# Time and channel mix on one core: sums and statistics of gathered rows behind the widening on VectorE

## The chip, the cores and the metric

The kernel runs on one core of a Trainium2 chip. A core has five engines that work side by side, each through its own queue in order: TensorE (PE in the profile, with its weight loads as PEld), VectorE (DVE), ScalarE (ACT), GpSimd (POOL) and SyncE (SP, which here only issues DMAs). They wait for each other through semaphores. The metric is the device time of one execution in microseconds (us), lower is better. About 0.2% of it (4.6 us) is what a measurement of this kernel can tell from no change.

## The reference

Two transformer-like layers over `x` of 32 sequences x 256 tokens x 128 channels, all float32, with a layer norm after each of the four parts: relative attention, a mixture of 14 routed and 2 shared experts (top 2), the time and channel mix, and attention over the sequence axis with a second mixture of 8 experts. The change lies in the third part, which with the norms around it is:

```python
x  = _layernorm(x + moe0(x))              # moe0's two routed rows per token are gathered and summed here
xn = _ln(x, ln1_g, ln1_b); xp = shift(xn)
k, v, r = mix(xn, xp) @ Wk, ... @ Wv, sigmoid(... @ Wr)
wkv = scan over the tokens: a = ew*a + exp(k)*v;  b = ew*b + exp(k);  a / (b + 1e-8)
y  = x + (r * wkv) @ Wo
yn = _ln(y, ln2_g, ln2_b)
kk = square(relu((0.5*yn + 0.5*shift(yn)) @ Wfk))   # 128 -> 512 channels: the widening
x  = _layernorm(x + y + sigmoid(yn @ Wfr) * (kk @ Wfv))  # 512 -> 128: the narrowing
```

## The kernel before

The phases run one after the other: `rel_attention`, `load_weights`, `moe0`, `rwkv`, `seq_attention`, `moe1`. The change is in `rwkv` (time and channel mix, from about 1243 us to about 1590 us of the profiled execution). It works on 8 units of 4 sequences, which are 1024 tokens or 8 tiles of 128 tokens each (`UB`, `UT`). In the code unit `i` is `q`, the next one is `ahead`, the one after it `third`. The next phase attends over the sequence axis, so it needs every unit of this one.

The order of the work is written out by hand: under `tc.manual_schedule` for PE, Pool, DVE and Activation, each engine executes its instructions in the order in which the loop at the end of `rwkv` issues them. So a line of that loop is a place in four queues at once. One iteration issues, with the lines of the code:

- `keys(ahead)`, `normed(q)`, `weigh(ahead)`, `values(ahead)`: mixing matmuls (L1419, L1420), exponentials, and on VectorE two scans (L1434, L1447) and a reciprocal of 6.5 us (L1450).
- `late(2)`, `scaled(third)`, `receive(ahead)`, `second(q)`: norm of the second half, transposes (L253), and two adds `ys` on GpSimd (L1487), from which the widening reads.
- `enter(third)`, `join(ahead)` (two VectorE operations, L1459, L1460), `gated(q)` (matmuls `ps_rr`, L1497).
- `late(3)`, then `widen(q)`.
- `settle(units[i - 1])`, `leave(ahead)`, `late(2)`, `narrow(q)`.

What these steps are made of:

- `late(n)` takes n steps of `taken_in()`, which has 51 steps: 18 are taken before the loop, 7 in each iteration, and they run out with the `late(3)` of iteration 4. Step k issues two gathers on GpSimd for row tile k (indirect DMAs, L935; each takes a place on GpSimd of about 1.3 us), then sums on VectorE the two rows of tile k-3 into X (two scalar_tensor_tensor, L1381). The last three steps have no gathers. After the eighth tile of a unit come its statistics: eight pairs of bn_stats and bn_aggr on VectorE (L1334, L1335, here called bn), then `sd_c` and `r_c` on GpSimd (L1336, L1337). In iterations 2, 3 and 4 these statistics fall into `late(3)`: after its first, second and third step. In iterations 0 and 1 they fall into the first `late(2)`.
- `widen(q)` issues an add X+y of 128x1024 on GpSimd (L1504), then eight times a matmul of the widening (`ps_kk`, L1510), a relu on ScalarE (L1515) and a square. The squares of the even blocks are on ScalarE (L1519), the four of the odd blocks on VectorE (L1517).
- `settle` finishes norms: for the unit before (`x`) and for a unit whose statistics are new (`c`), four small VectorE operations each (L1343 to L1348), of which the first, `shift_c`, needs `r_c` of GpSimd; then eight activations each on ScalarE (L1354) and a power on GpSimd (L1349).
- `leave(ahead)` has 8 matmuls `ps_o` (L1468), the add y = X + ps_o on VectorE (L1472, two operations of 128x512), and statistics of y. `narrow(q)` has 32 matmuls `ps_f` (L1527). Both write into the same two PSUM buffers (pool `r_o`), so `ps_f` can't start before L1472 has read `ps_o`. Behind `ps_f` come the gate (L1532), X (L1533), the statistics of x, and the next iteration's first scan on VectorE.

SyncE issues no DMA in this loop.

Of the kernel before, what the change touches and what calls it, by code (L numbers as in the profile page):

```python
# [30 lines left out]
class Kernel:  # L31
# [1237 lines left out]
    def rwkv(self):  # L1269
        nc, tc = self.nc, self.tc  # L1270
        UB, UT = 4, 8
        with ExitStack() as ctx:
# [44 lines left out]
            for i in range(B // UB):  # L1317
                q = Unit()
# [73 lines left out]
            def late(n):  # L1392
                for _ in range(n):
                    next(steps, None)

            def settle(q=None):
                if q is not None:
                    s = slice(UT * q.i, UT * (q.i + 1))
                    finish("x", q.x, q.x, q.last, self.scale2[:, s])
                while norms:  # L1400
                    i, stats = norms.pop(0)
                    x, s = units[i].x, slice(UT * i, UT * (i + 1))
                    finish("c", x, x, stats, self.scale1[:, s])
                    ready.add(i)

            def scaled(q):
                assert q.i in ready
                q.h = two.tile([P, UT, D], F32, tag="ln1", name="ln_h1", bufs=1)
                for t in range(UT):
                    s0 = UT * q.i + t  # L1410
                    nc.scalar.mul(q.h[:, t, :], q.x[:, t, :], self.scale1[:, s0 : s0 + 1])

            def enter(q):
                q.xn = turned(q.i, "xn", q.h, c["ln1_g"], c["ln1_b"])
# [8 lines left out]
            def keys(q):  # L1423
                q.ek = two.tile([P, UB, N], F32, tag="ek", name="ek")
                for u in range(0, UB, 2):
                    ps = mixdot(q, "k", u)
                    nc.scalar.activation(q.ek[:, u : u + 2, 1:], ps[:, :, 1:], AF.Exp)
                    nc.scalar.activation(
                        q.ek[:, u : u + 2, 0:1], ps[:, :, 0:1], AF.Exp, bias=c["time_first"]
                    )  # L1430

            def weigh(q):
                sb = q.sb = two.tile([P, UB, N], F32, tag="sb", name="sb")
                nc.vector.tensor_tensor_scan(  # L1434
                    flat(sb), flat(ew), flat(q.ek), 0.0, ALU.mult, ALU.add
                )
                nc.vector.tensor_scalar(sb, sb, 1e-8, None, ALU.add)

            def values(q):
                ekv = two.tile([P, UB, N], F32, tag="ekv", name="ekv")  # L1440
                for u in range(0, UB, 2):
                    ps = mixdot(q, "v", u)
                    nc.vector.tensor_tensor(
                        ekv[:, u : u + 2, :], q.ek[:, u : u + 2, :], ps, ALU.mult
                    )
                q.sa = two.tile([P, UB, N], F32, tag="sa", name="sa")
                nc.vector.tensor_tensor_scan(  # L1447
                    flat(q.sa), flat(ew), flat(ekv), 0.0, ALU.mult, ALU.add
                )
                nc.vector.reciprocal(q.sb, q.sb)  # L1450

            def receive(q):
                q.rr = two.tile([P, UB, N], F32, tag="rr", name="rr")
                for u in range(0, UB, 2):
                    ps = mixdot(q, "r", u)
                    nc.scalar.activation(q.rr[:, u : u + 2, :], ps, AF.Tanh, scale=0.5)

            def join(q):
                nc.vector.scalar_tensor_tensor(q.sa, q.rr, 1.0, q.sa, ALU.add, ALU.mult)  # L1459
                nc.vector.tensor_tensor(q.sa, q.sa, q.sb, ALU.mult)  # L1460

            def leave(q):
                y = q.y = two.tile([P, UT, D], F32, tag="y", name="y")
                for t0 in range(0, UT, 4):
                    ps = ps_o.tile([P, 4, D], F32, tag="o", name="ps_o")
                    for t in range(4):
                        b, f = divmod(t0 + t, 2)
                        nc.tensor.matmul(  # L1468
                            ps[:, t, :], q.sa[:, b, P * f : P * (f + 1)], wo,
                            start=True, stop=True,  # L1470
                        )
                    nc.vector.tensor_tensor(  # L1472
                        y[:, t0 : t0 + 4], q.x[:, t0 : t0 + 4], ps, ALU.add
                    )
                mv, r, shift = q.stats = statistics("y", y)
                nc.gpsimd.tensor_tensor(shift, mv[:, :, 0], r, ALU.mult)
                nc.gpsimd.tensor_scalar(shift, shift, -1.0, None, ALU.mult)

            def normed(q):
                q.h2 = two.tile([P, UT, D], F32, tag="ln2", name="ln_h2", bufs=1)  # L1480
                apply(q.h2, q.y, q.stats)
# [9 lines left out]
            def gated(q):  # L1491
                q.gate = two.tile([P, UT, D], F32, tag="gate", name="gate")
                for t0 in range(0, UT, 4):
                    ps = ps_o.tile([P, 4, D], F32, tag="o", name="ps_rr")
                    for t in range(4):
                        b, f = divmod(t0 + t, 2)
                        nc.tensor.matmul(  # L1497
                            ps[:, t, :], q.yn[:, b, 1 + P * f : 1 + P * (f + 1)], m["Wfr"],
                            start=True, stop=True,
                        )  # L1500
                    nc.scalar.activation(q.gate[:, t0 : t0 + 4], ps, AF.Tanh, scale=0.5)

            def widen(q):
                nc.gpsimd.tensor_add(q.x, q.x, q.y)  # L1504
                q.kks = []
                for u in range(0, UB, 2):
                    kk = two.tile([P, 4, 512], F32, tag="kk", name="kk")
                    for k in range(4):
                        ps = ps_m.tile([P, 2, N], F32, tag="m", name="ps_kk")
                        nc.tensor.matmul(  # L1510
                            ps, wfk[:, P * k : P * (k + 1)], q.ys[:, u : u + 2, :],
                            start=True, stop=True,
                        )
                        ps = ps.rearrange("p b t -> p (b t)")
                        nc.scalar.activation(kk[:, k, :], ps, AF.Relu)  # L1515
                        if k % 2:
                            nc.vector.tensor_tensor(kk[:, k, :], kk[:, k, :], kk[:, k, :], ALU.mult)  # L1517
                        else:
                            nc.scalar.activation(kk[:, k, :], kk[:, k, :], AF.Square)  # L1519
                    q.kks.append(kk)  # L1520
# [16 lines left out]
            with tc.manual_schedule(engines={E.PE, E.Pool, E.DVE, E.Activation}):  # L1537
                late(11)
                scaled(units[0])
                enter(units[0])  # L1540
                keys(units[0])
                weigh(units[0])
                late(2)
                values(units[0])
                receive(units[0])
                scaled(units[1])
                enter(units[1])
                join(units[0])
                late(2)
                leave(units[0])  # L1550
                late(3)
                settle()
                for i, q in enumerate(units):
                    ahead = units[i + 1] if i + 1 < len(units) else None
                    third = units[i + 2] if i + 2 < len(units) else None
                    if ahead:
                        keys(ahead)
                    normed(q)
                    if ahead:
                        weigh(ahead)  # L1560
                        values(ahead)
                    late(2)
                    if third:
                        scaled(third)
                    if ahead:
                        receive(ahead)
                    second(q)
                    if third:
                        enter(third)
                    if ahead:  # L1570
                        join(ahead)
                    gated(q)
                    late(3)
                    widen(q)
                    settle(units[i - 1] if i > 0 else None)
                    if ahead:
                        leave(ahead)
                    late(2)
                    narrow(q)
                settle(units[-1])  # L1580
# [539 lines left out]
```

## Time and profile before

| | us |
|---|---|
| median of 3 runs | 2285.38 |
| lowest, highest run | 2281.87, 2285.68 |
| profiled execution, its time | 2282.96 |
| profiled execution, its span | 2281.3 |

| engine | busy us (share of the span) |
|---|---|
| PE | 1878.6 (82%) |
| DVE | 1303.4 (57%) |
| ACT | 1089.7 (48%) |
| POOL | 874.5 (38%) |

Busy time by iteration of the loop, from the windows view (each begins at a first scan of VectorE, to about a microsecond). Iterations 5 and later have no gathers, sums or such statistics left.

| iteration | us | PE | DVE | ACT | POOL | granted PE clock |
|---|---|---|---|---|---|---|
| 0 | 50 | 33.50 | 38.30 | 23.86 | 34.76 | 0.83 |
| 1 | 48 | 33.15 | 37.71 | 24.77 | 33.87 | 0.86 |
| 2 | 41 | 33.55 | 36.58 | 25.60 | 32.26 | 0.92 |
| 3 | 40 | 32.55 | 35.03 | 24.32 | 32.84 | 0.91 |
| 4 | 42 | 32.47 | 36.61 | 25.10 | 22.18 | 0.92 |
| 5 | 32 | 30.44 | 27.91 | 22.00 | 12.52 | 1.00 |

A line of the timeline reads: start in us from the span's start, duration in us, engine, line of the code, operation, what it writes and reads, shape, count; in brackets the idle time of the engine before it and what ended it. Instructions of one kind that follow each other are merged into one line. A line of the windows view has the stretch, its length, then for each engine the busy time and, in parentheses, the number of instructions, then the granted PE clock as a share of full speed, and DMA.

### The profile page before, as it was taken

Reading aid. Unit: us, or ns where it says so; the run is one execution under the profiler, and the core shown is the slowest. Engines: PE = TensorE matmul, PEld = TensorE weight load, DVE = VectorE, ACT = ScalarE, POOL = GpSimd, SP = SyncE. Lnnn points to the kernel's source line nnn. Section 1 sums busy time; section 2 is a strip of 40 time slices with the busy share of each in tenths; the row PEclk is TensorE's granted clock in tenths of the full one; section 3 lists DMA queues with packets and bytes.
Section 4 is the critical chain, followed back from the end, with each engine's and each line's share of the span. In section 5 each row is a group of like instructions: output and inputs, shape, how many; then the busy total and the mean of one; then the engine's idle time right before and its main releaser. Section 6 shows DMA issues by size and latency. Waiting matters only on the chain.

```text
span 2281.3 us, 57436 instructions
## 1 busy us (share of the span) xinstructions
PE 1878.6 (82%) x22616; PEld 1492.9 (65%) x22616; DVE 1303.4 (57%) x4578; ACT 1089.7 (48%) x2438; POOL 874.5 (38%) x1047
## 2 busy tenths in 40 slices
PE   3899999999887995897998578887677777499795
PEld 2788887887776874676987345555455534399663
DVE  2465666666755655522423878986576535444575
ACT  1566665565554552332376346655576322244231
POOL 4000011002135423485056667744301165453775
PEclk9899999999999996899998789999798766599898
DMA  5121233101111102112453000001000000155221
GB/s 169 23 70 24 57 106 106 49 13 48 42 42 31 30 21 58 55 45 67 133 139 106 23 23 21 21 1 38 1 3 21 20 36 35 47 162 160 77 60 58
DMA packets 190957, 127.93 MB, mean 56 GB/s; under 512 B 54114, under 2 KB 179043, under 8 KB 189155
## 3 DMA queue, kind: packets, MB, share of 16 engines
q1 hardware_dynamic: 175074, 93.79, 14.2%
q0 software_dynamic: 14336, 29.39, 4.1%
q8 instruction: 182, 2.98, 0.5%
q10 hardware_dynamic: 1280, 1.08, 0.2%
q14 instruction: 85, 0.69, 0.1%
HBM read 61.27 MB, written 62.91 MB: 54 GB/s over the span
## 4 chain that ended last, share of the span: by engine, by line
PE 24%; DVE 16%; POOL 13%; issue 9%; DMA 5%; ACT 4%; another core or an unknown queue 1%; SPq 0%; POOLq 0%; DVEq 0%; ACTq 0%
POOL rows L925 4%; PE ps_sh L1009 3%; PE ps_sy L1022 3%; DMA gy<-results,at 3%; PE ps_f L1527 3%; POOL gy L935 2%; PE ps_s L1712 2%; DMA y<-results,at 1%; DVE sb L1450 1%; PE ps_t L543 1%; POOL y L935 1%; POOL rstd L171 1%; POOL xs L1099 1%; ACT pbuf L532 1%; PE sc L503 1%
## 5 line engine op out<-in xcount | busy, mean ns | idle before, releaser
L503 PE MATMUL sc<-ke,qt 64*64 64x256 f32 (+15 forms) x8192 | 359.3, 315 | 32.1 <-DMA qt<-qd 18.2
L503 PEld LDWEIGHTS sc<-ke,qt 64*64 64x64 f32 x8192 | 330.0, 205 | 75.1 <-issue 50.6
L532 ACT ACTIVATE pbuf<-pbuf,nb 128x256 f32<-128x256 f32 (+15 forms) x1024 | 313.5, 395 | 132.0 <-DVE nb L528 132.0
L528 DVE CUSTOM_DVE_ANT_0 pbuf<-sc,mask 128x256 f32<-128x256 f32 (+15 forms) x1024 | 229.9, 295 | 68.9 <-PE sc L503 49.3
L543 PE MATMUL ps_t<-ident,pbuf 128*128 128x128 f32 x1560 | 201.1, 280 | 21.4 <-ACT pt L132 10.0
L132 ACT COPY pt<-ps_t 128x512 f32<-128x512 f32 x195 | 113.9, 586 | 195.6 <-PE ps_t L543 184.9
L543 PEld LDWEIGHTS ps_t<-ident,pbuf 128*128 128x128 f32 x1560 | 172.9, 143 | 40.7 <-ACT pt L132 12.2
L134 DVE COPY pt<-ps_t 128x512 f32<-128x512 f32 x195 | 134.5, 691 | 72.5 <-PE ps_t L543 67.3
L1009 PE MATMUL ps_sh<-sxt,w1t 128*128 128x128 f32 x1088 | 139.2, 282 | 23.8 <-DVE sxt L981 10.8
L590 POOL TENSOR_TENSOR X<-X,r_L_attn_bp 128x2048 f32<-128x2048 f32 x4 | 18.3, 4564 | 365.6 <-PE ps_x L400 365.6
L759 ACT ACTIVATE hid<-ps_h 128x512 f32<-128x512 f32 x128 | 76.0, 597 | 162.7 <-PE ps_h L755 146.7
L925 POOL DMA_INDIRECT rows<-xs,where x128 | 125.4, 979 | 72.3 <-issue 37.4
L1009 PEld LDWEIGHTS ps_sh<-sxt,w1t 128*128 128x128 f32 x1088 | 130.4, 196 | 28.4 <-DVE sxt L981 11.4
L1014 ACT ACTIVATE shid<-ps_sh 128x512 f32<-128x512 f32 x136 | 81.0, 597 | 126.8 <-PE ps_sh L1009 108.4
L935 POOL DMA_INDIRECT gy<-results,at x96 | 94.7, 986 | 48.4 <-DMA sx<-rows 20.7
L925 POOL DMA_INDIRECT rows<-X,at x96 | 94.5, 985 | 29.1 <-issue 15.1
L556 PE MATMUL av<-pt,v 128*32 128x256 f32 (+1 forms) x2048 | 97.8, 332 | 7.6 <-DVE pt L134 6.9
L935 POOL DMA_INDIRECT y<-results,at x64 | 63.7, 995 | 104.3 <-DMA results<-sy 85.7
L914 POOL COPY at<-where 128x1 int32<-128x1 int32 x256 | 51.7, 203 | 121.9 <-DVE where L899 54.2
L580 DVE RECIPROCAL rc<-ps_c 128x16 f32<-128x16 f32 x64 | 16.4, 257 | 131.4 <-PE ps_c L577 131.4
L528 DVE DVE_READ_ACCUMULATOR2_ANT nb<- 128x1 f32 x1024 | 85.1, 83 | 0.0
L1527 PE MATMUL ps_f<-wfv,kk 128*128 128x128 f32 x512 | 65.9, 295 | 22.9 <-DVE y L1472 22.9
(355 smaller groups left out, 3966.2 us busy)
## 6 DMA issues: line engine op xcount, KB each, us to landing
sx<-rows SPq DMA_DIRECT2D x68, 256.0 KB
results<-sy SPq DMA_DIRECT2D x68, 256.0 KB
rows<-zero SPq DMA_DIRECT2D x10, 1024.0 KB
qt<-qpd SPq DMA_DIRECT2D x512, 8.0 KB
qd<-st SPq DMA_DIRECT2D x4, 1024.0 KB
qpd<-sp SPq DMA_DIRECT2D x4, 1024.0 KB
qt<-qd SPq DMA_DIRECT2D x256, 16.0 KB
kd<-st SPq DMA_DIRECT2D x4, 1024.0 KB
```

What stands on the lines that cost most here:

```text
L132: self.nc.scalar.copy(out, in_)
L134: self.nc.vector.tensor_copy(out, in_)
L503: nc.tensor.matmul(s.bank[i][64 * f : 64 * f + 64, off : off + w], lhs, rhs, start=key not in s.seen, stop=(1 - rows, g, f) in s.seen, ski ...
L528: nc.vector.tensor_tensor_reduce(out=pr, in0=s.bank[i][:, off : off + w], in1=mask[:, N - w : N], scale=-QS, scalar=3e38, op0=ALU.add, op1 ...
L532: last = nc.scalar.activation(pr, pr, AF.Exp, bias=nb, scale=-1.0)
L543: nc.tensor.transpose(ps[:, k, :], s.prob[:, at : at + P], ident)
L556: nc.tensor.matmul(av[32 * bl : 32 * bl + 32, bh, P * f :], v[:, 2 * b + f, 9 * s.h : 9 * s.h + 32], ptv[:, 32 * f : (32 if f == 0 else 48 ...
L925: i = nc.gpsimd.indirect_dma_start(rows, bass.IndirectOffsetOnAxis(ap=at, axis=0), src[:, n, :], None)
L935: self.nc.gpsimd.indirect_dma_start(out, None, rows, bass.IndirectOffsetOnAxis(ap=where, axis=0))
L1009: nc.tensor.matmul(ps[:, t, c, :], w1[t2 + t][:, P * c : P * (c + 1)], xt[:, t2 + t, :], start=True, stop=True,)
L1014: nc.scalar.activation(h.rearrange("p (t c) n -> p t c n", t=2), ps, func)
L1527: nc.tensor.matmul(ps[:, t, :], kk[:, k, P * t : P * (t + 1)], wfv[:, k, :], start=(k == 0), stop=(k == 3),)
```

## The change

In the loop at the end of `rwkv`, `late(3)` changes its place with `widen(q)`:

```diff
                     gated(q)
+                    widen(q)
                     late(3)
-                    widen(q)
                     settle(units[i - 1] if i > 0 else None)
                     if ahead:
                         leave(ahead)
```

Nothing is added or removed. On VectorE the sums (and in iterations 2, 3 and 4 the statistics) now stand behind the four squares and directly in front of `settle`. On GpSimd the add X+y (L1504) now stands directly behind the two `ys` adds, in front of the six gathers and of `sd_c` and `r_c`. PE's and ScalarE's queues keep their order, since `late` issues nothing on them.

## The prediction

> **What bounds it now.** I read the shares of the page, then the chain of waits between 1243 and 1336 us, then the timeline of each engine for iterations 0 to 5. Over the whole kernel PE is busiest, but in this loop the chain of waits goes through VectorE and from there into the narrowing. The page's groups say what its matmuls wait for:
>
> ```profile
> L1527 PE MATMUL ps_f<-wfv,kk 128*128 128x128 f32 x512 | 65.9, 295 | 22.9 <-DVE y L1472 22.9
> ```
>
> All their idle time is ended by y (L1472) on VectorE. So what counts is when L1472 starts: each us by which it is later makes the iteration longer by one, because `ps_f`, gate, X, statistics and the next scan follow it in one row. There are two kinds of iteration. VectorE, GpSimd and ScalarE in iteration 0:
>
> ```profile
> 1312.18 0.69 DVE L1517 TENSOR_TENSOR kk<-kk 128x512 f32<-128x512 f32 x1 [2.96 <-ACT kk L1515]
> 1315.05 0.69 DVE L1517 TENSOR_TENSOR kk<-kk 128x512 f32<-128x512 f32 x1 [2.17 <-ACT kk L1515]
> 1317.05 3.06 DVE L1517 TENSOR_TENSOR kk<-kk 128x512 f32<-128x512 f32 x2 [1.31 <-ACT kk L1515]
> ...
> 1320.59 1.28 DVE L1472 TENSOR_TENSOR y<-X,ps_o 128x512 f32<-128x512 f32 x2
> ```
> ```profile
> 1316.57 2.39 POOL L1504 TENSOR_TENSOR X<-X,y 128x1024 f32<-128x1024 f32 x1
> ```
> ```profile
> 1318.16 0.58 ACT L1515 ACTIVATE kk<-ps_kk 128x512 f32<-128x512 f32 x1
> ```
>
> Here VectorE idles in front of the squares (2.96 + 2.17 + 1.31 us), waiting for relus: the sums in front of them cost nothing. The third square (3.06 for two, against 0.69 for one) is held up until the GpSimd add ends at 1318.96. Iteration 1 is alike (idle 4.35, 2.16, 1.30; two squares 3.08). Iteration 2, VectorE, ScalarE, PE:
>
> ```profile
> 1398.40 0.73 DVE L1381 SCALAR_TENSOR_TENSOR X<-y,gate,X 128x128 f32<-128x128 f32 x2
> ...
> 1402.23 1.36 DVE L1381 SCALAR_TENSOR_TENSOR X<-y,gate,X 128x128 f32<-128x128 f32 x4
> 1403.51 2.49 DVE L1517 TENSOR_TENSOR kk<-kk 128x512 f32<-128x512 f32 x4
> 1405.91 0.16 DVE L1343 SCALAR_TENSOR_TENSOR shift_x<-mv_x,r_x 128x8 f32<-128x8 f32 x1
> ...
> 1407.02 1.28 DVE L1472 TENSOR_TENSOR y<-X,ps_o 128x512 f32<-128x512 f32 x2
> ```
> ```profile
> 1401.44 0.58 ACT L1515 ACTIVATE kk<-ps_kk 128x512 f32<-128x512 f32 x1
> ```
> ```profile
> 1407.75 9.75 PE L1527 MATMUL ps_f<-wfv,kk 128*128 128x128 f32 x64 [4.88 <-DVE y L1472]
> ```
>
> VectorE is never idle from its first scan to y; the relus are done (1402.02) before the squares begin. Iterations 3 and 4 are alike.
>
> **The change, part by part.** Moved are, in iterations 0 to 4: six sums on VectorE (1.95 us, from six in iteration 4, 1479.43 to 1481.38); in 2 to 4 also eight bn pairs (3.18 us, 1399.05 to 1402.23) and `sd_c`, `r_c` on GpSimd; in 0 to 3 six gathers. Four squares take 2.40 us in a row.
>
> *Iterations 0 and 1.* With the add out of the way, the last square waits only for the last relu (1318.16 + 0.58 = 1318.74) and is done at 1319.4, against 1320.04: 0.65 us gained. Then the sums, 1.95, now lie between squares and y: **+1.3**. In iteration 1 the last relu ends at 1366.55, the squares at 1367.2 (1367.87 before): again **+1.3**.
>
> *The add on GpSimd* goes to right behind the `ys` adds. In iterations 0 and 1 that is at 1308.7 and 1356.6, where VectorE idles: free. In 2, 3 and 4 it is at 1394.9, 1435.3 and 1475.9, where VectorE begins four sums and the join, all with two SBUF inputs like the held-up square. In iteration 0 a sum that met the `ys` adds took 1.96 us in place of 0.35. I take it that one sum waits out the add: the join ends 2.25 us later. The lower bound is no delay, if the add slips in behind the join.
>
> *Iteration 2.* Join done at 1398.40 + 2.25 = 1400.65, squares to 1403.05 (the last relu, 1402.02, is in time), two sums 1403.7, bn 1406.85, four sums 1408.15, four operations of settle for x 1408.7. `shift_c` waits for `r_c`: from the end of bn to the end of `r_c` it was 2.24 us (1402.23 to 1404.47; 2.78 in iteration 4, where squares ran beside it), so 1409.1. That wait is new; the squares covered it. Behind it in VectorE's queue stand the rest of settle (0.55) and y: 1409.7 against 1407.02, **+2.7**. Without the add's delay squares wait for relus, and it is +2.3.
>
> *Iteration 3.* Statistics after the second step, so less stands between them and `shift_c`: join 1441.0, squares 1443.4, four sums 1444.7, bn 1447.9, `r_c` 1450.1, y 1450.7 against 1447.41: **+3.3** (+2.9 without the delay).
>
> *Iteration 4.* No gathers; statistics at the very end. Before, the add held up a small operation of settle (L1348, 2.28 us in place of 0.17); that goes, and the sums pay instead. Join 1481.7, squares 1484.1, sums 1486.0, bn 1489.2, `r_c` 1491.45, y 1492.05 against 1490.15: **+1.9** (+1.45).
>
> *The gathers* come one add (2.4 us) later, in iteration 2 the last four behind the late `r_c` (about 1409.3 to 1414.1, before 1404.7 to 1409.5). The first sum that reads these rows would be at about 1414.8; a row landed about 1.5 us behind its gather in iteration 0 (1305.34 to 1306.85), so they are there. On GpSimd behind them: `r_y` and `shift_y` by 1420.2, which ScalarE wants at about 1424.3; then four gathers to 1425.2, and the next `sd_x` is held up by the scan until 1427.0 anyway, as before. Were this cover (1.8 us) gone, `ys` and the widening would be late by as much. SyncE's queue has nothing here.
>
> *Sum of the order:* 1.3 + 1.3 + 2.7 + 3.3 + 1.9 = **+10.5 us** (9.25 if the add is not in the way).
>
> *PE's clock.* In iterations 0 and 1 `ps_f` ran at full clock (7.42 us) behind idle gaps of 1.72 and 2.29 us. These grow to 3.0 and 3.6. The windows view, in pairs of neighbouring stretches:
>
> ```profile
> 863.10:866.50 3.40, 0.48 (x16) 0.13 (x4) 1.30 (x14) 3.40 (x13) 0.00 (x0) 1.00 0.00 0
> 866.50:869.90 3.40, 3.22 (x15) 3.22 (x16) 1.24 (x3) 0.43 (x2) 0.00 (x0) 0.51 0.00 0
> 1149.90:1153.30 3.40, 1.51 (x13) 1.51 (x14) 0.00 (x0) 2.15 (x6) 1.95 (x2) 1.00 0.33 96
> 1153.30:1156.70 3.40, 3.40 (x18) 3.40 (x18) 1.19 (x4) 2.56 (x7) 2.32 (x4) 0.50 0.23 67
> ...
> 1368.30:1371.70 3.40, 2.00 (x18) 2.00 (x18) 3.16 (x15) 3.40 (x10) 3.12 (x2) 1.00 0.00 0
> 1371.70:1375.10 3.40, 3.40 (x33) 3.40 (x32) 3.19 (x14) 2.62 (x7) 1.66 (x3) 1.00 0.00 0
> ```
>
> A stretch with PE busy for 0.48 or 1.51 us is followed by half clock; one with 2.00 (the gap of iteration 1) is not. The Trainium skill, "TensorE: Matmul & The Clock Gate", section "What's actually happening", says that the clock halves after an idle window of about 3.4 us, with windows that run freely. By that rule a gap of 3.0 us never fills a window and one of 3.6 hardly ever: cost 0, sum 10.5. By the rows partly busy windows are enough: in this trace all nine gaps of 2.7 to 6 us that began at full clock were followed by half clock, and of seven of 1.9 to 2.1 us three were. I go by the rows: both `ps_f` fall. The price is between 1.7 (3.4 us at half rate) and 2.6 (`ps_f` took 9.17, 9.75 and 10.03 in iterations 4, 2, 3); I take 2.0 each, **+4.0**. The widening's matmuls in 2 to 4 start behind gaps of 2.04 to 2.07 us and kept full clock three times; the squares now follow the relus closely, so a fall costs 1.7 less a slack of 0.4 (last relu at 1402.0, its square due at 1402.45). With three of seven such gaps falling, one of these three is likeliest: **+1.3**, ends 0 and 3.9.
>
> **Total:** 10.5 + 4.0 + 1.3 = **+15.8**. On the profiled execution (span 2281.3 and 1.7 around it: 2282.96) that is 2298.8. This execution lies 2.4 below the median of 2285.38 and inside the runs' spread; on the spread's middle, 2284, it is **2300**.
>
> **The rivals.**
> - *The clock holds* (26%): the order costs 9.25 to 10.5 and no fall is added: 2294. For it: the page's rule. Against: the nine gaps.
> - *Only places change* (10%): in iterations 2 to 4 VectorE was full, and swapping what fills it moves y by nothing; iterations 0 and 1 remain, +2.6, 2287, no change that can be told. For it: no idle time there. Against: it needs `r_c` in time, and squares, sums, bn and settle give no cover of 2.24 us after bn.
> - *The sums leave the path* (4%): faster. If y is issued without the sums and statistics in front of it, L1472 stands right behind squares and settle: by the same times -0.65 twice, -2.8, -2.9 and -4.9, together -12, and three `ps_f` behind gaps of about 2 us keep full clock, -6.6: 2266 to 2272. It decides where VectorE takes y ahead of sums that were issued before it. Against: in every iteration its order is the written one, and y starts within 0.1 us of the operation written before it.
> - *GpSimd late too* (8%): widening falls to half clock in two or three iterations, or gathers push `ys` back: 2304 to 2310.
>
> The forecast, order and both falls, +12 to +19, has 52%. Slower are it, the first and the last rival: 86%; same 10%, faster 4%. The range 2289 to 2307 leaves out the second and third rival and the top of the last.
>
> **What would show it.** Squares behind the join with 2.4 us in a row in iterations 2 to 4, a first sum of over 2 us beside L1504, no square above 0.7 us; `shift_c` idle for 0.4, 1.0 and 1.7 us behind `r_c`; gaps before `ps_f` of about 3.0, 3.6, 7.6, 8.2, 8.9; `ps_f` above 9 us in iterations 0 and 1. The prediction is wrong if y starts no later behind the join than before, or if `ps_f` no longer waits for y.

## The result, and the profile after

The changed kernel takes 2295.37 us (median of 5 runs, 2290.15 to 2300.93), the kernel before 2285.38 (5 runs, 2280.10 to 2286.76). The ratio is 1.0054, with a 95% interval of 1.0037 to 1.0072: slower by about half a per cent. The profiled execution of the changed kernel took 2290.15 us, its span is 2287.6.

The narrowing's group on the profile page, after; its idle time in front was 22.9 us before:

```profile
L1527 PE MATMUL ps_f<-wfv,kk 128*128 128x128 f32 x512 | 66.7, 297 | 32.5 <-DVE y L1472 32.5
```

In front of the narrowing PE waits 9.6 us longer, and for nothing but y. The windows view of the changed kernel, one line for each of iterations 0 to 4, cut at the first scan (L1434) of each:

```profile
1280.40:1331.74 51.34, 34.61 (x147) 24.05 (x146) 35.28 (x84) 22.47 (x50) 33.55 (x29) 0.80 0.09 24
1331.74:1383.17 51.43, 35.31 (x153) 22.87 (x152) 35.69 (x90) 25.26 (x58) 34.19 (x27) 0.83 0.07 18
1383.17:1425.31 42.14, 31.97 (x153) 21.39 (x152) 38.05 (x90) 24.99 (x58) 31.19 (x26) 0.92 0.07 20
1425.31:1469.49 44.18, 33.84 (x153) 22.25 (x152) 38.15 (x90) 25.15 (x58) 32.34 (x29) 0.88 0.08 24
1469.49:1514.06 44.57, 33.66 (x153) 22.05 (x152) 36.97 (x86) 25.23 (x58) 21.89 (x17) 0.89 0.02 6
```

The same five were 48.62, 48.38, 40.39, 40.66 and 41.89 us before. Together, called **the loop** from here on, they are 233.66 us against 219.94: **+13.7**. Iterations 5 and later are the same (iteration 5 takes 31.91 in both). The profiled execution as a whole grew by only 7.2 us in time and 6.3 in span: its loop began 4.3 us earlier, and what follows the last `ps_f` took 3.1 less. No instruction outside the loop was changed, and runs of the kernel before alone differ by 6.7 us, so I read the change from the loop. The ratio's interval, 8.5 to 16.5 us, holds the loop's 13.7 as well as the 10.0 between the medians.

The loop's chain adds up in both kernels. In each of the five iterations `ps_f` starts 0.73 to 0.74 us after y, and the next first scan 4.54 to 4.55 us after `ps_f` ends. So an iteration is longer by just what y starts later and `ps_f` takes longer.

VectorE in iteration 0, after ("..." marks lines left out):

```profile
1312.59 0.71 DVE L1517 TENSOR_TENSOR kk<-kk 128x512 f32<-128x512 f32 x1 [1.13 <-ACT kk L1515]
1314.31 0.69 DVE L1517 TENSOR_TENSOR kk<-kk 128x512 f32<-128x512 f32 x1 [1.00 <-ACT kk L1515]
1314.92 2.03 DVE L1381 SCALAR_TENSOR_TENSOR X<-y,gate,X 128x128 f32<-128x128 f32 x6
...
1317.42 1.28 DVE L1472 TENSOR_TENSOR y<-X,ps_o 128x512 f32<-128x512 f32 x2
```

The squares are no longer held up by GpSimd's add (0.71, 0.69), but the six sums, which stood in idle time before, now lie between them and y. Iteration 2, VectorE:

```profile
1396.04 3.86 DVE L1381 SCALAR_TENSOR_TENSOR X<-y,gate,X 128x128 f32<-128x128 f32 x4
...
1402.21 2.49 DVE L1517 TENSOR_TENSOR kk<-kk 128x512 f32<-128x512 f32 x4
1404.61 0.73 DVE L1381 SCALAR_TENSOR_TENSOR X<-y,gate,X 128x128 f32<-128x128 f32 x2
...
1410.71 0.17 DVE L1343 SCALAR_TENSOR_TENSOR shift_c<-mv_c,r_c 128x8 f32<-128x8 f32 x1 [0.35 <-POOL r_c L1337]
...
1411.27 1.28 DVE L1472 TENSOR_TENSOR y<-X,ps_o 128x512 f32<-128x512 f32 x2
```
PE in iteration 0 before, then in iterations 0, 2 and 3 after:

```profile
1321.32 7.41 PE L1527 MATMUL ps_f<-wfv,kk 128*128 128x128 f32 x64 [1.72 <-DVE y L1472]
```
```profile
1318.16 9.04 PE L1527 MATMUL ps_f<-wfv,kk 128*128 128x128 f32 x64 [3.02 <-DVE y L1472]
...
1412.01 8.76 PE L1527 MATMUL ps_f<-wfv,kk 128*128 128x128 f32 x64 [7.61 <-DVE y L1472]
...
1437.58 8.83 PE L1510 MATMUL ps_kk<-ys,w_L_attn_Wfk 128*128 128x512 f32 x16 [2.04 <-POOL ys L1487]
```

Four sums of `late(2)` take 3.86 us in place of 1.56: the first (2.82 us) ends with the add X+y on GpSimd. `shift_c` waits 0.35 us for `r_c` (0.99 and 1.56 in iterations 3 and 4). `ps_f` of iteration 0, at full clock before, fell to half clock behind a gap of 3.02 us, and so did the widening in iterations 3 and 4 (8.83 us; 7.13 before). The windows view around two of these bursts, after, and around `ps_f` of iteration 2 before:

```profile
1315.88:1319.29 3.41, 1.13 (x10) 1.13 (x11) 3.24 (x13) 2.23 (x6) 1.67 (x1) 1.00 0.00 0
1319.29:1322.70 3.41, 3.41 (x19) 3.41 (x18) 3.13 (x17) 0.96 (x3) 0.65 (x2) 0.50 0.00 0
...
1408.04:1414.86 6.82, 2.85 (x13) 2.86 (x14) 6.01 (x30) 4.95 (x13) 5.05 (x6) 0.50 0.07 20
```
```profile
1405.85:1412.68 6.83, 4.93 (x23) 4.93 (x24) 6.38 (x30) 6.26 (x16) 6.02 (x5) 0.50 0.13 38
```

In iteration 0 the half clock lasted 3.41 us, all of it inside `ps_f`. In iteration 2 it lasted 6.8 us in both kernels, but PE worked in 4.93 us of it before and in 2.85 after, since y came later; `ps_f` took 9.75 and 8.76 us.

### The profile page after: what moved, and what is told of

The parts are those of the page before. It is cut to its first block, busy times and chain, and to the rows that moved or that the text cites. A ratio compares the mean times of both kernels' runs of the same rounds, so it can differ in the third digit from the quotient of the medians.

```text
span 2287.6 us, 57433 instructions
## 1 busy us (share of the span) xinstructions
PE 1875.9 (82%) x22616; PEld 1489.6 (65%) x22616; DVE 1302.1 (57%) x4578; ACT 1090.0 (48%) x2438; POOL 873.7 (38%) x1047
## 4 chain that ended last, share of the span: by engine, by line
PE 26%; POOL 14%; DVE 14%; issue 9%; DMA 5%; ACT 4%; another core or an unknown queue 1%; SPq 0%; POOLq 0%; DVEq 0%; ACTq 0%
POOL rows L925 4%; PE ps_sh L1009 3%; PE ps_sy L1022 3%; DMA gy<-results,at 3%; PE ps_f L1527 2%; DMA y<-results,at 2%; POOL y L935 2%; PE ps_s L1712 2%; PE ps_h L755 2%; PE ps_y L767 2%; PE ps_t L543 1%; PE sc L503 1%; POOL rstd L171 1%; PE ps_kk L1510 1%; POOL xs L1099 1%
## 5 line engine op out<-in xcount | busy, mean ns | idle before, releaser
L503 PE MATMUL sc<-ke,qt 64*64 64x208 f32 (+15 forms) x8192 | 358.1, 315 | 31.9 <-DMA qt<-qd 17.6
L543 PEld LDWEIGHTS ps_t<-ident,pbuf 128*128 128x128 f32 x1560 | 171.8, 142 | 40.6 <-ACT pt L132 12.3
L1527 PEld LDWEIGHTS ps_f<-wfv,kk 128*128 128x128 f32 x512 | 65.3, 212 | 34.3 <-DVE y L1472 33.9
```

The costliest lines, as they stand in the source:

```text
L503: nc.tensor.matmul(s.bank[i][64 * f : 64 * f + 64, off : off + w], lhs, rhs, start=key not in s.seen, stop=(1 - rows, g, f) in s.seen, ski ...
L543: nc.tensor.transpose(ps[:, k, :], s.prob[:, at : at + P], ident)
L1527: nc.tensor.matmul(ps[:, t, :], kk[:, k, P * t : P * (t + 1)], wfv[:, k, :], start=(k == 0), stop=(k == 3),)
```

## The experiments

All are edits of the loop in `rwkv`. Chips differ: the kernel before took 2292.9 (one run), 2245.1 and 2297.1 us (medians) beside the experiments, so a time is compared only with the kernel before on the same chip, and mechanisms are read from the loop's parts. Loops can be compared between chips: iteration 5, which has no gathers and sums left, took 31.84 to 31.91 us in each of the first six runs below and 31.91 in both kernels. The first four and the second run with PE kept busy are one execution each; in the order below they took 2.5, 18.0, 12.4, 22.0 and 9.2 us more than the kernel before on their chip, with loops longer than the 219.94 of the profile before by 2.4, 20.3, 6.8, 17.6 and 6.2. Line numbers shift by a few in the edited kernels.

### The add alone

```diff
  # in the kernel before; total() holds the add X+y of widen()
                     gated(q)
+                    total(q)
                     late(3)
                     widen(q)
```

> The kernel before, with GpSimd's add X+y (L1504) alone moved in front of late(3); sums and statistics stay in front of the squares. I read the loop from the first scan of iteration 0 to that of iteration 5: 219.9 us before, 233.7 changed. My theory (the sums' place in front of y costs, the add only shifts where VectorE is held up): y 0.65 us earlier in iterations 0 and 1, 2.3 later in 2 and 3, 0.2 later in 4; loop 221 to 224, ps_f at full clock in 0 and 1 (7.4 us). Rival (the slowdown comes from the add that now blocks sums and join): most of it is here, loop 230 or more.

Measured: loop 222.35. Against the kernel before y starts 1.15 and 0.61 us earlier in iterations 0 and 1, later by 2.28, 2.30 and 0.18 in 2, 3 and 4 (all from the iteration's first scan). Of the 1.15, 0.50 is a widening that took 9.58 us in place of 10.08. `ps_f` keeps 7.41 us in 0 and 1. VectorE in iteration 2:

```profile
1392.27 3.86 DVE L1381 SCALAR_TENSOR_TENSOR X<-y,gate,X 128x128 f32<-128x128 f32 x4
...
1407.05 1.28 DVE L1472 TENSOR_TENSOR y<-X,ps_o 128x512 f32<-128x512 f32 x2
```

The held-up sum is here as in the changed kernel, but no wait stands between squares and y. The add's new place alone costs 2.4 us of loop, against 13.7 for the whole change; the rival that it is the cause falls.

### The squares alone

```diff
  # in the changed kernel
                     widen(q)                  # without the add
                     late(3)
+                    total(q)
```

> The other half of the change: squares in front of sums and statistics, but the add X+y (L1504) stays behind the gathers. My theory: y later than before by 1.95 us in iterations 0 and 1 (the add again holds up a square), 2.3 in 2, 2.9 to 4 in 3, about 3.6 in 4 (the add holds up settle); ps_f falls to half clock in 0 and 1 (9 us); loop 231 to 236 against 233.7 of the changed kernel. Rival (the add is the cause): loop 220 to 224.

Measured: loop 240.24, more than either theory said. y came later than before by 1.93, 1.95, 3.99, 6.52 and 3.61 us. Iterations 0, 1 and 4 are as expected; VectorE in 0:

```profile
1313.91 3.21 DVE L1519 TENSOR_TENSOR kk<-kk 128x512 f32<-128x512 f32 x2 [1.16 <-ACT kk L1521]
```

The add holds up a square again. In iteration 2 the widening fell to half clock (8.83 us). In iteration 3 GpSimd came late: its `ys` adds began 13.3 us after the scan, not 11.2 as in every other iteration from 2 on of this run, and the widening, behind a gap of 4.17 us, ran at half clock too. So the order costs without the add's new place too. Whether that place made the change cheaper isn't shown: of the 6.6 us by which this loop is longer than the changed kernel's, 4.65 lie in iterations 2 and 3, where the clock and GpSimd's lateness differ.

### Without the wait for r_c in front of y

```diff
  # in the changed kernel; settle(q, False) leaves the c part out
-                    settle(units[i - 1] if i > 0 else None)
+                    settle(units[i - 1] if i > 0 else None, False)
                     if ahead:
                         leave(ahead)
+                    settle()
```

> The changed kernel, with the c part of settle (shift_c and three more, which wait for r_c) put behind leave(ahead), so that y waits neither for r_c nor for these operations. My theory: y earlier than in the changed kernel by 0.55, 0.55, 0.95, 1.55 and 2.25 us in iterations 0 to 4, loop about 228; 225 if the shorter gaps keep ps_f of 0 and 1 at full clock. Rival (the wait for r_c is hidden, only four small operations move): 0.55 in each, loop about 231.

Measured: loop 226.76. Against the changed kernel y was earlier by 0.53, 1.15, 1.04 and 3.48 us in iterations 0, 1, 2 and 4, and 0.25 later in 3, where GpSimd again came late by 2.1 us. In 1 the widening took 0.6 us less than in the changed kernel, which is the rest of the 1.15; in 4 it did not fall, which is 1.2 of the 3.5. `ps_f` in iterations 0 and 1, PE:

```profile
1320.99 7.41 PE L1527 MATMUL ps_f<-wfv,kk 128*128 128x128 f32 x64 [2.46 <-DVE y L1472]
1369.64 9.04 PE L1527 MATMUL ps_f<-wfv,kk 128*128 128x128 f32 x64 [3.01 <-DVE y L1472]
```

A gap of 2.46 us kept full clock, one of 3.01 didn't. The wait for `r_c` and the four operations behind it are on the path.

### PE kept busy in front of the narrowing

```diff
  # in the changed kernel; n matmuls that nobody reads
                     late(2)
+                    warm = ps_m.tile([P, 2, N], F32, tag="m", name="ps_warm")
+                    for _ in range(n[i]):          # cut: only in iterations 0 to 4
+                        nc.tensor.matmul(warm, wfk[:, 0:P], q.ys[:, 0:2, :], start=True, stop=True)
                     narrow(q)
```

> The changed kernel, with 5, 6, 14, 14, 15 matmuls of 128x512 between ps_o and ps_f in iterations 0 to 4, whose result nobody reads: PE isn't idle in front of ps_f. VectorE's order is that of the changed kernel. My theory: ps_f runs at full clock, 7.4 us in place of 9.04 in 0 and 1 and of 8.8 to 8.9 in 2 to 4, loop about 226.5. Rival (the half clock has nothing to do with the gap before ps_f, or costs nothing since VectorE is busy meanwhile): loop stays at 233 to 235.

Measured: loop 237.51, a miss of my own making. I had counted about 0.43 us for a matmul; one of 128x512 in float32 shows as two instructions and takes about 0.88 (eight in 7.03 us, below). So they ended after y and kept `ps_f` from starting, by 1.1 us in iteration 0 and 4.2 in 2. `ps_f` itself took 7.31 us in all five. Again with 3, 3, 8, 8, 9:

> As the run with matmuls between ps_o and ps_f, but 3, 3, 8, 8, 9 of them in iterations 0 to 4: one took about 0.86 us, so that they end before y starts (gaps of 3.0, 3.6, 7.6, 7.8, 8.4 us in the changed kernel). My theory: ps_f follows y by 0.7 us and takes 7.4 us in all five, so the loop is 233.7 less 1.6 twice, 1.35, 1.5 and 1.35, about 226, with one or two falls of the widening's clock as before. Rival (the half clock in front of ps_f costs nothing on the path): loop 232 to 235.

Measured: loop 226.11. PE in iteration 2, then GpSimd in iteration 3:

```profile
1408.62 7.03 PE L1582 MATMUL ps_warm<-ys,w_L_attn_Wfk 128*128 128x512 f32 x16
1416.40 7.41 PE L1527 MATMUL ps_f<-wfv,kk 128*128 128x128 f32 x64 [0.75 <-DVE y L1472]
```
```profile
1432.79 2.07 POOL L1336 TENSOR_SCALAR sd_x<-mv_x 128x8 f32<-128x8 f32 x1
...
1441.68 2.04 POOL L1487 TENSOR_TENSOR ys<-yn 128x512 f32<-128x512 f32 x2
```

All five `ps_f` take 7.41 us, 7.5 us less in sum than in the changed kernel. In iterations 0 and 2, where y starts 0.11 us earlier and 0.02 later, `ps_f` is shorter by 1.63 and 1.35 and the iteration by 1.74 and 1.32: the half clock is real time on the path. That the whole loop is 7.55 us less is partly luck. In iteration 3 y came 2.2 us later, behind a late GpSimd; in 1 and 4 it came 0.95 and 1.21 earlier, behind a shorter widening (9.24 for 10.20, and no fall). The GpSimd lines show what "late" means above: `sd_x` began 4.43 us after the scan (0.17 to 3.17 in the changed kernel), behind the moved gathers, and `ys` 13.3 after it, not 11.2. That iteration took 44.82 us, the one before it 40.81.

### late(3) behind y as a whole

```diff
  # in the changed kernel
                     widen(q)
-                    late(3)
-                    settle(units[i - 1] if i > 0 else None)
+                    settle(units[i - 1] if i > 0 else None, False)
                     if ahead:
                         leave(ahead)
+                    late(3)
                     late(2)
                     narrow(q)
+                    settle()
```

> late(3) as a whole moved further, behind leave(ahead): squares, four operations of settle, y, statistics of y, then sums and new statistics, late(2), narrow, and the c part of settle behind narrow. My theory: y comes earlier than before by about 1.2 us in iterations 0 and 1 and 3.4 to 5.5 in 2 to 4, ps_f keeps full clock; but sums and statistics now stand between y and gate on VectorE, longer than ps_f takes, so that some of it is given back: loop 210 to 219 against 219.9 before, time 2275 to 2285. Rival (the amount of VectorE's work sets the iteration, its order nothing): loop 219 to 222.

Measured: 2272.39 us against 2245.11 of the kernel before on that chip, ratio 1.0115 (1.0099 to 1.0131); loop 247.78. y came early, in iterations 2 to 4 by more than expected, since `ys` began 7.3 to 8.6 us after the scan, not 11.2 (1.5, 1.7, 5.9, 5.9 and 8.0 us before its time in the kernel before), and `ps_f` took 7.41 us, but all was given back and more. VectorE in iteration 0, behind y:

```profile
1307.58 0.35 DVE L1381 SCALAR_TENSOR_TENSOR X<-y,gate,X 128x128 f32<-128x128 f32 x1 [3.76 <-DMA y<-results,where]
...
1322.25 2.29 DVE L1434 TENSOR_TENSOR_SCAN sb<-ew,ek 128x1024 f32<-128x1024 f32 x1 [4.08 <-ACT ek L1428]
```

I had moved ten gathers into one row on GpSimd, behind its norm of y, and the sums of `late(2)` then wait for rows just asked for (3.76, 0.92, 0.86 and 0.96 us). `shift_c`, now behind the statistics of x (at 1317.55), makes ScalarE's eight activations late, and the exponentials behind them, on which the scan waits (4.08). The rival, that VectorE's amount of work alone sets the iteration, falls as well. A step that is moved takes its DMAs along.

### Only the statistics behind y

```diff
  # in the kernel before; reckon() holds the statistics that late() issued
                     gated(q)
                     late(3)                   # sums and gathers, no statistics
                     widen(q)                  # without the add X+y
-                    settle(units[i - 1] if i > 0 else None)
+                    settle(units[i - 1] if i > 0 else None, False)
+                    total(q)
                     if ahead:
                         leave(ahead)
+                    reckon()
                     late(2)
                     narrow(q)                 # with settle() in front of the statistics of x
```

The c part of `settle` and the add move with them.

> The kernel before, with only the statistics of gathered rows (eight bn pairs, sd_c, r_c) taken out of late, in the loop always behind leave(ahead), the c part of settle behind the last X of narrow, and the add X+y behind the x part of settle. Sums stay in front of the squares, where they fill the wait for relus. My theory: in iterations 2 to 4 y is about 3.8 us earlier than before and ps_f keeps full clock; in 0 and 1, GpSimd's ys adds no longer queue behind r_c, so PE's gap in front of the widening (4.5 and 12 us) shrinks to about 2: iterations of 37 to 40 us, loop 185 to 200 against 219.9, time 2255 to 2268. Rival (what moves behind y comes back in full between y and the next scan): iterations 2 to 4 stay at 40 to 42, loop 205 or more.

Measured: 2229.05 us against 2245.11, ratio 0.9922 (0.9907 to 0.9937); loop 191.94. The stretch from the first scan of all to that of iteration 0, however, took 41.85 us in place of 30.89, since there I had put the statistics behind six gathers. The repaired version keeps them where they were in front of the loop, and puts the add of iteration 0 in front of `late(3)`:

> As the run with statistics behind y, with two repairs: in front of the loop the statistics stay inline (deferred, their r_c came behind six gathers and the first scan of iteration 0 10.9 us late), and in iteration 0 the add X+y goes in front of late(3) (behind it, it held up six sums for 2.7 us). My theory: from the first scan to that of iteration 0 30.9 us again in place of 41.9, iteration 0 at about 37 in place of 39.8, loop about 189; ratio to before about 0.986. Rival (the prologue's loss is hidden by something else): ratio stays at 0.992.

Measured: 2269.66 us (6 runs) against 2297.10 (11 runs), ratio **0.9888** (0.9861 to 0.9916): 27 us faster than the kernel before. The stretch in front is 30.5 us; the loop 193.27, for iteration 0 took 42.8 where I had said 37 (ScalarE waits 5.99 us for a scale on GpSimd behind four gathers, and then `ys` and the add hold up sums, 6.00 us for four). VectorE and PE in iteration 2:

```profile
1381.80 2.03 DVE L1381 SCALAR_TENSOR_TENSOR X<-y,gate,X 128x128 f32<-128x128 f32 x6
1383.74 2.54 DVE L1526 TENSOR_TENSOR kk<-kk 128x512 f32<-128x512 f32 x4
...
1386.75 1.28 DVE L1479 TENSOR_TENSOR y<-X,ps_o 128x512 f32<-128x512 f32 x2
...
1398.27 0.22 DVE L1343 SCALAR_TENSOR_TENSOR shift_c<-mv_c,r_c 128x8 f32<-128x8 f32 x1
...
1403.00 2.29 DVE L1441 TENSOR_TENSOR_SCAN sb<-ew,ek 128x1024 f32<-128x1024 f32 x1 [0.85 <-ACT ek L1435]
```
```profile
1387.48 7.41 PE L1536 MATMUL ps_f<-wfv,kk 128*128 128x128 f32 x64 [1.21 <-DVE y L1479]
```

The sums stay in front of the squares, where they cover the wait for relus; the statistics run beside `ps_f`; y starts 21.7 us after the scan (25.4 before), `ps_f` keeps full clock, and VectorE is idle for 0.85 us in 38. In iteration 1, `ys` no longer queues behind `r_c` and comes 11.2 us after the scan, not 21.2: it takes 38.0 us in place of 48.4. Of the loop's gain of 26.7 us, 1.4 are given back from iteration 5 to the last `ps_f` (81.6 us; 80.2 before). What each of the three moved parts is worth by itself was not run.

## Why the prediction was right

The direction, the mechanism of the order and the range held; 2300 was forecast, 2295.4 measured, +15.8 against +10.0 by the medians and +12.3 by the ratio. The two terms of the clock were off in opposite directions. By its own steps, with y measured from the iteration's first scan in the two profiles:

| step | predicted us | measured us |
|---|---|---|
| y later, iterations 0, 1, 2 | 1.3, 1.3, 2.7 | 1.10, 1.42, 2.74 |
| y later, iterations 3, 4 (without the widening's fall) | 3.3, 1.9 | 3.39, 1.88 |
| sum of the order | 10.5 | 10.5 |
| `ps_f` at half clock, iterations 0 and 1 | 4.0 | 3.26 |
| `ps_f` in 2 to 4 | 0 | -2.48 |
| widening at half clock | 1.3 (one fall) | 2.4 (two falls) |
| loop | 15.8 | 13.7 |

*The order.* The delay by the add (2.25 predicted, 2.29 measured for the join in iteration 2), the sums and statistics in front of y, and `shift_c` waiting for `r_c` (0.4, 1.0, 1.7 predicted; 0.35, 0.99, 1.56) came as worked out. In iterations 3 and 4 y is later by 4.59 and 3.08; 1.2 of each is the widening's fall, by which the last square comes later (22.05 us after the scan; 20.84 in iteration 2, where it kept full clock). The runs that kept PE busy have the same order on VectorE: where their widening did not fall (iteration 3 of the first, 4 of the second), y was later by 3.43 and 1.87. In iterations 0 and 1 the widening runs partly at half clock and took 8.57 to 10.20 us over the two kernels and the first five experiments, by which y moves too. Counted from the end of the widening, y is 1.30 and 1.28 us later (4.07 and 4.62 us behind it, before 2.77 and 3.34), as predicted; 1.10 and 1.42 are what the widening makes of it in these two executions (9.89 for 10.08, 10.20 for 10.06). The runs with the add alone and without the wait for `r_c` show two of the terms one at a time.

*The clock.* Between the rows and the rule the rows were right: `ps_f` fell behind gaps of 3.02 and 3.56 us, which by the rule of the Trainium skill ("TensorE: Matmul & The Clock Gate", "What's actually happening": one idle window of about 3.4 us, running freely) would seldom or never halve the clock. These runs don't agree with it: in the 3.41 us in front of iteration 0's half clock PE was busy for 1.13. Over all runs the five gaps in front of `ps_f` between 3.0 and 4.5 us in iterations 0 and 1 all fell, while 2.46 and less kept full clock. The mis-sized term is the price: 1.63 each, not 2.0, and I had left the other three `ps_f` at what they took. In the 21 `ps_f` of iterations 0 to 4 that fell, over all runs, the time above 7.41 us is 0.47 to 0.48 of the half-clock time in which `ps_f` worked (2.86 to 5.82 us); half clock that passes while PE is idle adds nothing. In this loop it came in stretches of 3.41 us or a multiple, and how much of one was left when y came differed: in the three runs before the one with PE kept busy, `ps_f` of iterations 2 to 4 took 8.86 to 10.17 us behind gaps of 6.2 to 10.6, in sum 0.6 to 1.8 us less than in the kernel before. So the clock came to +0.8 in place of +4.0 because the half clock that was already there overlapped more with waiting; how much more is partly luck of this execution. That half clock itself costs the path is shown by the run that kept PE busy.

*The gathers.* In the changed kernel they were covered, as said. The cover of 1.8 us is as thin as it was said to be: in three experiments with the changed kernel's gathers it was gone in iteration 3, and `ys` came 2.1 us later.

*The rivals.* "The clock holds" and "only places change" fell with the rows above. Of "GpSimd late too" one half came true, since the widening fell in two iterations, but that cost 2.4 us, and the time stayed below its 2304. The faster rival, sums that leave the path, needed an order that the change doesn't have; moved there in full it was slower still, as gathers and `shift_c` came late, and with the statistics moved, together with the c part of `settle` and the add, it was faster by 1.1%.

What stays open is why the profiled execution won 7 us outside the loop; medians and ratio leave room for it to be spread between runs, but that wasn't tested.

## What to carry to other kernels

In queues ordered by hand, ask of each block what it covers where it stands: here, in two iterations, sums filled a wait for relus at no cost, and behind it they delayed the one instruction that another engine waited for. Move what has time (statistics, whose result is read an iteration later) behind that instruction, and leave what fills a gap. Count what goes along in the other engines' queues: an add or a gather that the move carries to a new place can hold up work there that has nothing to do with it.

## What the hardware showed beside that

The length of an idle gap of PE did not tell what a fall costs: `ps_f` took 8.94 us behind 7.81 us of idle time in the changed kernel and 9.91 behind 7.82 in the run with the squares alone, where it worked at half clock for 3.23 and 5.28 us. The widening behind gaps of 2.02 to 2.13 us fell in 5 of 19 cases over all runs, so runs of one kernel can differ by this alone. And in iterations 2 to 4 GpSimd's lateness came in a step: with `sd_x` starting anywhere up to 3.2 us behind VectorE's scan, `ys` began 11.2 us after it; starting at 4.4, 13.3. Why it is a step stays open.
